# Layer two's second pass: one group of attention products for a block's four tiles in place of two groups for two tiles each

## The chip, the cores and the metric

The kernel runs on one core of one Trainium2 chip. The metric is the device time of one execution in microseconds; the time before is 2650.01 us, the median of three runs (2649.26 to 2651.77).

## What is computed

Two layers of an attention over small graphs: 128 graphs of S = 64 nodes with H = 768 features, all in float32.

```python
h = jnp.maximum(_layernorm(x), 0.0)
temper = sqrt(H)
for l in range(2):
    m_left  = einsum('bsh,oh->bso', h, W_left[l])
    m_right = einsum('bsh,oh->bso', h, W_right[l])
    u_left, u_right = h @ m_left.T / temper, h @ m_right.T / temper
    u = u_left * adj_tri + u_left * diag_mask + u_right * swapaxes(adj_tri, 1, 2)
    e = exp(u) * adj
    attention = e / (sum(e, axis=2) + 1e-10)
    h_lin = einsum('bsh,oh->bso', h, W_lin[l]) + b_lin[l]
    ctx = attention @ h_lin
    h = relu((ctx - mean(ctx)) / (std(ctx, ddof=1) + 1e-3) * ln_a[l] + ln_b[l])
out = x + h
```

## The kernel before

Each layer has two passes. The first makes the scores and the attention. The second, `pass_two`, makes `h_lin`, the attention products, the normalisation and, in layer two, the residual sum and the output. The change is in layer two's second pass.

**Blocks.** The 8192 rows are worked on in 16 blocks u of 512 rows: four tiles of 128 rows, called (r, k) with r and k 0 or 1, two graphs to a tile. `h_lin` of a block is computed by a bilinear scheme with fewer products than the plain one: 15 products (`ORDER`), each of eight matmuls of 128x128 by 256 columns (`multiply`, L1006). Their operands are sums of blocks of the weights, prepared once, and sums of blocks of the tokens (`T_SUMS`, 11 for each block, made on GpSimd at L245 for the next block).

**Banks and reads.** The products go to four PSUM banks named X, Y, Z and V. `NAME` turns them from one use to the next, so that the tile that TensorE's rows call Z can be the bank "X" of the order. Several products accumulate in one bank, and after each of them the running sum is read out into one or two of the six parts of the tile `hl`: the first read of a part is a copy on ScalarE (L300), every later one an addition on VectorE (L245, `hl<-hl,bank`). Products 0, 2, 4, 6, 8 and 10 share one bank, so each of them waits for the reads of the one before it there. Product 8 has two reads, both on VectorE. Four of the banks are loaded beforehand with the bias by ScalarE (`fresh`, L995).

**Order of the work.** Each engine has its own instruction stream in program order. All other work is hung on numbered slots: `put(n, f)` hangs a step on slot n, and `linear` runs slot 2i in the middle of product i and slot 2i + 1 behind its reads. Slots beyond 29 are carried into the next block, less 30. On the slots of a block u in layer two lie: the affine steps of the next block on ScalarE (L379, slots 9 to 14), the token sums of the next block on GpSimd (slots 15 to 27), and the finish of the block before. Block 15 is different: its products are run for tiles of r = 0 and then again for r = 1, with four matmuls each and 30 slots to each half.

**The finish before.** `finish(u, r)` finishes two tiles. `context` issues 16 matmuls of 64x64 by 384 columns (L1048) into two pairs of PSUM banks, `aux`. ScalarE squares both tiles with a running sum (L1193) and takes the root (L1195). Then come, on slots: `inverse` (VectorE, L1198 and L1199); `scaled` for each tile, a multiply by 1/deviation and by `a` on VectorE (L1203) and an addition of `b` on GpSimd (L1206); and `done` for each tile, a VectorE operation on two operands in SBUF, max(z, 0) + x (L1217), with two stores to the output on SP's queue (L1219). The rows of x come by `residual`, four loads on SP's queue (L1133) into two of four buffers `xr`. In blocks 1 to 14 of layer two the calls for (u - 1, 0) and (u - 1, 1) stand behind products 0 and 7, with their steps on slots 6 to 12 and 20 to 30.

**Layer one's finish.** `finish_block(u, more)` finishes all four tiles behind product 12. `context_block` issues 16 matmuls, eight of 512 and eight of 256 columns (L1071), into the `aux` banks and into two of the product banks. The two parts in product banks are copied to SBUF by VectorE (L1143), which frees them for the next block. Squares, deviation, inverse and scaled come on slots 25 to 36; in layer one scaled is on ScalarE (L1168), and the rows are then stored, with no done step.

`finish_last` makes the last two tiles of all, and `last_block` prepares rows for them, among others a negated `b` on GpSimd (L1093).

Of the kernel before, what the change touches and what calls it, by code (L numbers as in the profile page):

```python
# [12 lines left out]
AF = mybir.ActivationFunctionType  # L13
ALU = mybir.AluOpType
# [3 lines left out]
def kernel(  # L18
# [48 lines left out]
    def put(slot, *fs):  # L67
        plan.setdefault(slot, []).extend(fs)
# [943 lines left out]
    def pass_two(l, aside):  # L1012
        last = l == L - 1
        with tc.tile_pool(name=f"two{l}", bufs=2, reuse_waits="tile") as sp, \
# [59 lines left out]
            def batch(r, k, h):  # L1074
                return 4 * (h if k == 0 else 1 - h) + r + 2 * k
# [59 lines left out]
            def finish_block(u, more):  # L1135

                parts = context_block(u)
                tiles = ((0, 0), (0, 1), (1, 0), (1, 1))
                zs = {t: sp.tile([P, H], F32, name="z", bufs=4) for t in tiles}
                cut = (slice(0, T), slice(T, H))  # L1140

                for t in ((1, 1), (1, 0)):
                    nc.vector.tensor_copy(zs[t][:, cut[0]], parts[t][0])  # L1143
                    parts[t][0] = zs[t][:, cut[0]]
                    if t == (1, 1):
                        AHEAD.append(fresh(l, 0, more))
                ss = stat.tile([P, Q, 2], F32, name="ssb", bufs=2)
                sd = stat.tile([P, Q], F32, name="sdb", bufs=2)
                rs = stat.tile([P, Q], F32, name="rsb", bufs=2)

                def squares(t):
                    junk = zs[0, t[1]]
                    for n in range(2):
                        nc.scalar.activation(junk[:, cut[n]], parts[t][n], AF.Square,
                                             accum_out=ss[:, 2 * t[0] + t[1], n:n + 1])

                def deviation():
                    nc.vector.reduce_sum(sd, ss, axis=mybir.AxisListType.X)
                    nc.scalar.activation(sd, sd, AF.Sqrt, bias=floor, scale=1.0 / (H - 1.0))

                def inverse():
                    nc.vector.tensor_scalar_add(rs, sd, EPS_LN)
                    nc.vector.reciprocal(rs, rs)

                def scaled(t):
                    by = rs[:, 2 * t[0] + t[1]:2 * t[0] + t[1] + 1]
                    for n in range(2):
                        nc.scalar.activation(zs[t][:, cut[n]], parts[t][n], AF.Copy, scale=by)  # L1168
                    kept(u, *t, zs[t])

                order = ((1, 1), (1, 0), (0, 0), (0, 1))
                for f, slots in ((squares, (25, 26, 28, 29)), (scaled, (33, 34, 35, 36))):
                    for n, t in zip(slots, order):
                        put(n, lambda f=f, t=t: f(t))
                put(30, deviation)
                put(32, inverse)

            def kept(u, r, k, z):
                for h in range(PAIR):
                    nc.sync.dma_start(ROWS[u][batch(r, k, h)], z[h * S:(h + 1) * S])  # L1180

            def finish(u, r):

                cx = context(u, r)
                zs = [sp.tile([P, H], F32, name="z", bufs=4) for _ in range(2)]
                if last and not u and not r:
                    residual(u, r)
                two = "p (n d) -> p n d"
                ss = stat.tile([P, 2], F32, name="ss", bufs=2)
                sd = stat.tile([P, 2], F32, name="sd1", bufs=2)  # L1190
                rs = stat.tile([P, 2], F32, name="rs1", bufs=2)
                for k in range(2):
                    nc.scalar.activation(zs[k].rearrange(two, n=2), cx[k], AF.Square, accum_out=ss[:, k:k + 1])  # L1193

                nc.scalar.activation(sd, ss, AF.Sqrt, bias=floor, scale=1.0 / (H - 1.0))  # L1195

                def inverse():
                    nc.vector.tensor_scalar_add(rs, sd, EPS_LN)  # L1198
                    nc.vector.reciprocal(rs, rs)  # L1199

                def scaled(k):
                    if last:
                        nc.vector.scalar_tensor_tensor(  # L1203
                            zs[k].rearrange(two, n=2), cx[k], rs[:, k:k + 1],
                            rows["a"].rearrange(two, n=2), op0=ALU.mult, op1=ALU.mult)
                        nc.gpsimd.tensor_add(zs[k], zs[k], rows["b"])  # L1206
                        return
                    if (u, r, k) == (NB - 1, 1, 1):
                        nc.vector.tensor_scalar_mul(zs[k].rearrange(two, n=2), cx[k], rs[:, k:k + 1])
                    else:  # L1210
                        nc.scalar.activation(zs[k].rearrange(two, n=2), cx[k], AF.Copy, scale=rs[:, k:k + 1])
                    kept(u, r, k, zs[k])

                def done(k):
                    if last:
                        xs = XS[u, r]
                        nc.vector.scalar_tensor_tensor(xs[k], zs[k], 0.0, xs[k], op0=ALU.max, op1=ALU.add)  # L1217
                        for h in range(PAIR):
                            nc.sync.dma_start(out[u * NBB + batch(r, k, h)], xs[k][h * S:(h + 1) * S])  # L1219
                        if k and u + r < NB - 1 and (u, r) != (NB - 2, 0):  # L1220
                            residual(u + r, 1 - r)

                steps = [lambda f=f, k=k: f(k) for f in (scaled, done) for k in range(2)]
                return [inverse] + (steps if last else steps[:2])

# [35 lines left out]
            for u in range(NB):  # L1261
                turn = not last and u >= NB - 2
                put(4, lambda u=u: load_at(u))
                if u + 1 < NB:
                    load_h(2, l, u + 1, u == 0)
                    put_all(9 if u else 15, affine(2, l, u + 1))
                    put_sums_t((2, l, u + 1), 15 if u else 21, 1, 0)
                    if turn:
                        load_rows(1, 0, sp)
                        put_all(10, transpose_rows(1, 0, sp), 2)  # L1270
                        put(27, lambda: load_rows(1, 1, sp))
                    if u == 1 and not last:
                        sums_ahead(1, extra, 3)
                    assert not turn or not background
                    if u in aside:
                        aside[u]()
                    ends = {}
                    if u and last:
                        ends = {0: ((u - 1, 0), (6, 7, 8, 11, 12)), 7: ((u - 1, 1), (20, 21, 22, 30, 30))}
                    elif u > NB - 3:  # L1280
                        ends = {5: ((u - 1, 0), (16, 17, 18)), 11: ((u - 1, 1), (28, 29, 30))}
                    elif u:
                        ends = {12: (u - 1, None)}
                    linear(u, (0, 1), 0, ends, (0, 1) if u + 2 < NB else (0,))
                    for n in sorted(plan):
                        plan[n - 30] = plan.pop(n)
                else:
                    if turn:
                        load_h(1, 1, 0)
                        put_all(24, transpose_rows(1, 1, sp), 2)  # L1290
                        put_all(2, [fetch.popleft() for _ in range(8)], 2)
                        put_all(46, [lambda: TOKENS[1].step(0)] * Tokens.LIMIT, 1)
                        put(48, lambda: load_h(1, 1, 1))
                        put_all(28, affine(1, 1, 0), 3)
                        ends = ({1: ((u - 1, 0), (13, 14, 16)), 11: ((u - 1, 1), (34, 35, 36))},
                                {4: ((u, 0), (50, 51, 52))})
                    else:
                        last_block(u)
                        put(8, lambda: residual(u - 1, 1))
                        ends = ({0: ((u - 1, 0), (12, 13, 15, 19, 31)), 9: ((u - 1, 1), (28, 29, 30, 39, 41))},  # L1300
                                {2: ((u, 0), (44, 48, 51, 61, 62))})
                    linear(u, (0,), 0, ends[0], (1,))
                    linear(u, (1,), 30, ends[1], ())
                    for n in sorted(plan):
                        run(n)
                    for f in (finish_last if last else finish)(u, 1):
                        f()
# [57 lines left out]
```

## Time and profile before

| what | value |
|---|---|
| time, median of 3 runs | 2650.01 us |
| the profiled execution | 2648.42 us, of which 2646.6 us are the span from first to last instruction |
| granted TensorE clock, mean | 0.995 |
| busy: TensorE, VectorE, ScalarE, GpSimd | 2591.6, 1780.6, 935.4, 1763.1 us |
| layer two's second pass on TensorE | from about 2156 us to the end |

How rows are read: PE is TensorE, DVE VectorE, ACT ScalarE, POOL GpSimd, SP the engine whose queue issues DMAs. In a timeline a row has the start and the length in us, engine, line of the program, operation, out<-in, partitions x elements, the number of instructions merged in the row, and in brackets how long the engine had been idle before it and what ended that. In a group, `a/b/c` are the shortest, median and longest duration in ns.

### The profile page before, as it was taken

What the parts mean: (1) busy time and instruction counts of PE and PEld (TensorE: products, weight loads), DVE (VectorE), ACT (ScalarE), POOL (GpSimd) and SP (SyncE); (2) the same over time, 40 slices, a digit from 0 to 9 for tenths busy, and PEclk for the clock granted to TensorE, in tenths of its full rate; (3) what the DMA queues carried; (4) which work ended last, traced back from release to release, by engine and by line L of the source; (5) the groups of instructions that cost most, each with busy time, mean ns of one, the idle gap of its engine ahead of it and who ended that gap; (6) DMA issues with size and microseconds to landing.
All of it is one profiled execution on the core that took longest, in us unless ns stands there. A gap on an engine that the chain in (4) does not pass through costs nothing. (4 is left out here: it accounts for less than half of the span.)

```text
span 2646.6 us, 47202 instructions
## 1 busy us (share of the span) xinstructions
PE 2591.6 (98%) x18122; PEld 2217.1 (84%) x18122; DVE 1780.6 (67%) x2888; ACT 935.4 (35%) x1969; POOL 1763.1 (67%) x1392
## 2 busy tenths in 40 slices
PE   9899999999999999999999999999999989999998
PEld 8788888888888888888798888888888878887886
DVE  7878787777768445554456667677666676666667
ACT  5522223223113244454542222122222335555453
POOL 4766676666668657676276666667666657878786
PEclk9999999999999999999999999999999999999999
DMA  7443534343421354445794424253532215555655
GB/s 220 113 111 86 124 93 110 93 119 79 98 60 56 123 156 149 159 139 182 219 282 101 121 68 108 71 129 93 136 98 70 67 49 157 157 167 166 177 161 146
DMA packets 258465, 331.84 MB, mean 125 GB/s; under 512 B 56002, under 2 KB 190402, under 8 KB 258242
## 3 DMA queue, kind: packets, MB, share of 16 engines
q1 hardware_dynamic: 241442, 320.56, 44.3%
q10 hardware_dynamic: 16800, 8.26, 1.2%
q8 instruction: 145, 2.38, 0.4%
q14 instruction: 78, 0.64, 0.1%
HBM read 213.39 MB, written 115.34 MB: 124 GB/s over the span
## 5 line engine op out<-in xcount | busy, mean ns | idle before, releaser
L245 POOL TENSOR_TENSOR g<-ht 128x512 f32<-128x512 f32 (+1 forms) x620 | 785.9, 1279 | 420.8 <-PE Z L702 71.6
L245 POOL TENSOR_TENSOR g<-g,g 128x512 f32<-128x512 f32 (+1 forms) x310 | 397.9, 1291 | 136.7 <-PE C L702 22.0
L245 POOL TENSOR_TENSOR g<-ht,g 128x512 f32<-128x512 f32 (+1 forms) x272 | 346.1, 1282 | 164.8 <-PE Z L702 42.8
L702 PE MATMUL X<-g,g 128*128 128x256 f32 (+1 forms) x1080 | 252.9, 377 | 6.0 <-DVE m L914 6.0
L1006 PE MATMUL Z<-g,g 128*128 128x256 f32 x1024 | 244.1, 380 | 3.5 <-ACT hl L300 3.2
L702 PE MATMUL C<-g,g 128*128 128x256 f32 x1008 | 239.7, 381 | 4.9 <-POOL g L245 2.2
L702 PEld LDWEIGHTS X<-g,g 128*128 128x128 f32 x1080 | 203.0, 191 | 34.8 <-DVE m L914 6.8
L702 PE MATMUL Y<-g,g 128*128 128x256 f32 (+1 forms) x968 | 225.7, 376 | 3.8 <-POOL g L245 3.8
L1006 PEld LDWEIGHTS Z<-g,g 128*128 128x128 f32 x1024 | 191.6, 190 | 35.8 <-issue 4.1
L379 ACT ACTIVATE ht<-ht,b_col,a_col 128x256 f32<-128x256 f32 x384 | 196.1, 591 | 69.0 <-DMA ht<-h 53.8
L702 PEld LDWEIGHTS C<-g,g 128*128 128x128 f32 x1008 | 190.5, 190 | 32.9 <-POOL g L245 3.5
L702 PE MATMUL Z<-g,g 128*128 128x256 f32 (+1 forms) x936 | 217.0, 375 | 0.0
L702 PE MATMUL D<-g,g 128*128 128x256 f32 x880 | 209.8, 381 | 1.8 <-POOL g L245 1.8
L702 PEld LDWEIGHTS Y<-g,g 128*128 128x128 f32 x968 | 182.0, 190 | 27.8 <-POOL g L245 4.2
L702 PE MATMUL V<-g,g 128*128 128x256 f32 (+1 forms) x840 | 194.6, 375 | 3.1 <-POOL g L245 1.6
L702 PEld LDWEIGHTS Z<-g,g 128*128 128x128 f32 x936 | 174.5, 190 | 23.1
L702 PEld LDWEIGHTS D<-g,g 128*128 128x128 f32 x880 | 168.1, 191 | 25.7 <-POOL g L245 2.5
L1006 PE MATMUL X<-g,g 128*128 128x256 f32 x768 | 182.7, 379 | 0.0
L702 PEld LDWEIGHTS V<-g,g 128*128 128x128 f32 x840 | 157.6, 191 | 23.3 <-POOL g L245 1.7
L1206 POOL TENSOR_TENSOR z<-z,b 128x768 f32<-128x768 f32 x62 | 112.7, 1829 | 81.7 <-DVE z L1203 77.2
L245 DVE TENSOR_TENSOR m<-m,Y 128x512 f32<-128x512 f32 (+2 forms) x196 | 126.5, 667 | 58.4 <-ACT m L910 35.7
L245 DVE TENSOR_TENSOR m<-m,D 128x512 f32<-128x512 f32 x180 | 118.2, 677 | 70.0 <-ACT m L910 51.3
(222 smaller groups left out, 4612.0 us busy)
## 6 DMA issues: line engine op xcount, KB each, us to landing
ht<-h SPq DMA_DIRECT2D x126, 768.0 KB, 6.3
h<-xb SPq DMA_DIRECT2D x124, 384.0 KB, 6.6
z<-z SPq DMA_DIRECT2D x128, 192.0 KB, 3.1
x<-z SPq DMA_DIRECT2D x128, 192.0 KB, 5.4
xr<-in_x_dram SPq DMA_DIRECT2D x120, 192.0 KB, 3.8
out_dram<-xr SPq DMA_DIRECT2D x120, 192.0 KB, 2.7
x<-in_x_dram SPq DMA_DIRECT2D x112, 192.0 KB, 5.4
g<-form SPq DMA_DIRECT2D x40, 256.0 KB, 5.6
```

Source lines behind the costliest of these rows:

```text
L245: (eng.tensor_add if sign == "+" else eng.tensor_sub)(o, a, b)
L379: nc.scalar.activation(ht, ht, AF.Relu, bias=cols[1][:, c:c + 1], scale=cols[0][:, c:c + 1])
L702: nc.tensor.matmul(o, w[:, c, g * P:(g + 1) * P], t, start=(new and g == c == at == 0), stop=(c == K2 - 1), skip_group_check=True)
L1006: nc.tensor.matmul(p[:, n], b[t][:, c, r * P:(r + 1) * P], w[s][:, c, :], start=(i in FIRST and i not in PRELOAD and n == c == 0), stop=(c ...
L1206: nc.gpsimd.tensor_add(zs[k], zs[k], rows["b"])
```

## The change

In layer two, blocks 0 to 13 are finished by `finish_block` behind product 12 of the following block, as in layer one. `finish_block` gets layer two's steps: scaled is two VectorE operations a tile (512 and 256 columns) with `a`, followed by the addition of `b` on GpSimd, at slots 33, 35, 37 and 39; done is at slots 39, 41, 43 and 45, in the order (1,1), (1,0), (0,0), (0,1). The residual rows are loaded at slots 21 (r = 1) and 22 (r = 0) of the block that holds the group, and no longer inside `finish`. Block 14 is still finished by two calls of `finish` within block 15, now behind products 8 and 13 of its first half in place of 0 and 9, with other slots. Layer one is untouched.

```diff
@@ finish_block
+                def done(t):
+                    z, xs = zs[t], XS[u, t[0]][t[1]]
+                    nc.vector.scalar_tensor_tensor(xs, z, 0.0, xs, op0=ALU.max, op1=ALU.add)
+                    for h in range(PAIR):
+                        nc.sync.dma_start(out[u * NBB + batch(*t, h)], xs[h * S:(h + 1) * S])
+
                 def scaled(t):
                     by = rs[:, 2 * t[0] + t[1]:2 * t[0] + t[1] + 1]
                     for n in range(2):
-                        nc.scalar.activation(zs[t][:, cut[n]], parts[t][n], AF.Copy, scale=by)
-                    kept(u, *t, zs[t])
+                        if last:
+                            nc.vector.scalar_tensor_tensor(zs[t][:, cut[n]], parts[t][n], by, rows["a"][:, cut[n]],
+                                                           op0=ALU.mult, op1=ALU.mult)
+                        else:
+                            nc.scalar.activation(zs[t][:, cut[n]], parts[t][n], AF.Copy, scale=by)
+                    if last:
+                        nc.gpsimd.tensor_add(zs[t], zs[t], rows["b"])
+                    else:
+                        kept(u, *t, zs[t])
 
                 order = ((1, 1), (1, 0), (0, 0), (0, 1))
-                for f, slots in ((squares, (25, 26, 28, 29)), (scaled, (33, 34, 35, 36))):
+                steps = ((scaled, (33, 35, 37, 39)), (done, (39, 41, 43, 45))) if last else ((scaled, (33, 34, 35, 36)),)
+                for f, slots in ((squares, (25, 26, 28, 29)),) + steps:
@@ finish
-                if last and not u and not r:
-                    residual(u, r)
...
-                        if k and u + r < NB - 1 and (u, r) != (NB - 2, 0):
-                            residual(u + r, 1 - r)
@@ pass_two, blocks 1 to 14
                     if u and last:
-                        ends = {0: ((u - 1, 0), (6, 7, 8, 11, 12)), 7: ((u - 1, 1), (20, 21, 22, 30, 30))}
-                    elif u > NB - 3:
+                        for r in (1, 0):
+                            put(22 - r, lambda u=u, r=r: residual(u - 1, r))
+                    if u > NB - 3 and not last:
                         ends = {5: ((u - 1, 0), (16, 17, 18)), 11: ((u - 1, 1), (28, 29, 30))}
                     elif u:
                         ends = {12: (u - 1, None)}
@@ pass_two, block 15
                         last_block(u)
-                        put(8, lambda: residual(u - 1, 1))
-                        ends = ({0: ((u - 1, 0), (12, 13, 15, 19, 31)), 9: ((u - 1, 1), (28, 29, 30, 39, 41))},
+                        put(12, lambda: residual(u - 1, 0))
+                        put(17, lambda: residual(u - 1, 1))
+                        ends = ({8: ((u - 1, 0), (19, 20, 22, 26, 27)), 13: ((u - 1, 1), (31, 32, 34, 39, 41))},
                                 {2: ((u, 0), (44, 48, 51, 61, 62))})
```

## The prediction

> **What bounds the kernel now.** I read the page first, then TensorE's timeline over one block of layer two's second pass, then the same stretch on VectorE, GpSimd and ScalarE, and last a block of layer one's second pass, which already has the single group.
>
> ```profile
> PE 2591.6 (98%) x18122; PEld 2217.1 (84%) x18122; DVE 1780.6 (67%) x2888; ACT 935.4 (35%) x1969; POOL 1763.1 (67%) x1392
> ```
>
> TensorE is 98% busy, so only two things move the time: shorter TensorE work, or a new TensorE wait. One block (u around 10) of layer two on TensorE, first column the start, second the length:
>
> ```profile
> 2339.34 1.89 PE L1006 MATMUL Z<-g,g 128*128 128x256 f32 x8
> 2341.16 1.52 PE L1048 MATMUL aux<-hl,at 64*64 64x384 f32 x16
> 2342.61 1.99 PE L1006 MATMUL V<-g,g 128*128 128x256 f32 x8
> 2344.44 1.89 PE L1006 MATMUL Z<-g,g 128*128 128x256 f32 x8
> ...
> 2353.07 1.89 PE L1006 MATMUL X<-g,g 128*128 128x256 f32 x8
> 2354.89 1.52 PE L1048 MATMUL aux<-hl,at 64*64 64x384 f32 x16
> 2356.34 1.99 PE L1006 MATMUL Z<-g,ht 128*128 128x256 f32 x8
> 2358.17 1.89 PE L1006 MATMUL Y<-g,ht 128*128 128x256 f32 x8
> 2359.90 1.89 PE L1006 MATMUL Z<-g,g 128*128 128x256 f32 x8
> ...
> 2370.35 1.52 PE L1048 MATMUL aux<-hl,at 64*64 64x384 f32 x16
> ```
>
> No row has an idle time behind it: the pass is dense. Five products lie between 2344.44 and 2353.07, so one takes 1.726 us. The block repeats after 2370.35 - 2341.16 = 29.19 us; less 15 products that leaves 3.30 us for its two attention calls.
>
> **What is removed: TensorE time.** The single group as layer one runs it:
>
> ```profile
> 1087.06 1.89 PE L1006 MATMUL Y<-g,g 128*128 128x256 f32 x8
> 1088.88 0.65 PE L1071 MATMUL X<-hl,at 64*64 64x512 f32 x2
> ...
> 1089.79 1.90 PE L1071 MATMUL aux<-hl,at 64*64 64x256 f32 x24
> 1091.62 1.99 PE L1006 MATMUL V<-g,g 128*128 128x256 f32 x8
> 1093.45 1.89 PE L1006 MATMUL Y<-g,g 128*128 128x256 f32 x8
> ```
>
> From 1087.06 to 1093.45 are two products and the group: 6.39 - 3.45 = 2.94 us. It saves 3.30 - 2.94 = 0.36 us in each of the 14 blocks finished so (u = 0 to 13): **-5.0 us**. That is all the gain there is.
>
> **What moves: VectorE's part.** Before, a block's two scaled steps and two done steps come twice, in two places. Now four scaled come at slots 33 to 39 and four done at 39 to 45, that is at slots 3 to 15 of the block after the one that holds the group, without a pause. The rows that price them:
>
> ```profile
> 2348.77 1.94 DVE L1203 SCALAR_TENSOR_TENSOR z<-aux,rs,a 128x768 f32<-128x768 f32 x2
> 2351.62 0.69 DVE L245 TENSOR_TENSOR hl<-hl,Y 128x512 f32<-128x512 f32 x1 [0.91 <-PE Y L1006]
> 2352.22 4.00 DVE L1217 SCALAR_TENSOR_TENSOR xr<-z,xr 128x768 f32<-128x768 f32 x2
> 2358.45 1.29 DVE L245 TENSOR_TENSOR hl<-hl,Z 128x512 f32<-128x512 f32 x2 [2.23 <-PE Z L1006]
> L1217 DVE SCALAR_TENSOR_TENSOR xr<-z,xr x60: 951/2023/2432, 2206.2 to 2626.0; 128x768 f32<-128x768 f32 x60
> 2349.86 3.60 POOL L1206 TENSOR_TENSOR z<-z,b 128x768 f32<-128x768 f32 x2 [3.77 <-DVE z L1203]
> 2353.93 3.42 POOL L245 TENSOR_TENSOR g<-ht 128x512 f32<-128x512 f32 x2 [0.47 <-ACT ht L379]
> 2357.43 1.27 POOL L245 TENSOR_TENSOR g<-g,ht 128x512 f32<-128x512 f32 x1
> ```
>
> A done step needs 0.951 us alone (shortest of 60) but 2.02 in the median. The rows show why. The first was issued at 2352.22 while GpSimd's second z add ran (2349.86 + 3.60 = 2353.46); the sum that GpSimd began at 2353.93 then took far longer than 1.27, and the two dones ended at 2356.22. Taking turns gives just that: done from 2353.46 for 0.81, sum 1.13, done 0.81 = 2356.21. So where both queue, a done costs 0.81 plus what GpSimd has in hand: 1.13 for a sum, 1.68 for a z add. Steps with one operand in PSUM do not take part: scaled, L1203, is 1.94 for two beside an add, a read 0.69 beside a sum.
>
> The deadline is read 8. Products 8 and 10 accumulate in one bank, with both of product 8's reads on VectorE between them. Before, product 8 ends at 2358.17 (where product 9 starts), its two reads run 2358.45 to 2359.74, and product 10 starts at 2359.90: 0.16 us to spare, and VectorE had been idle 2.23 us.
>
> Now the chain after the change, from the start of a block's product 0, with 0.23 us from the end of a product to its read (the rows have 0.2 to 0.28), VectorE's next start 0.08 before the last end, and shorter pieces priced by two rows of a read:
>
> ```profile
> 2611.99 0.75 DVE L245 TENSOR_TENSOR hl<-hl,Z 128x256 f32<-128x256 f32 x2
> 2612.85 0.42 DVE L245 TENSOR_TENSOR hl<-hl,Y 128x256 f32<-128x256 f32 x1
> ```
>
> 0.69 at 512 columns and 0.42 at 256 is 0.27 for 256, so scaled in two pieces steps on by 0.66 + 0.40 us a tile from PSUM; the bottom tiles' first piece, copied to SBUF, by 0.60 (0.95 less 0.27, less 0.08).
> - Product 1 ends at 3.45, its read frees VectorE at 4.28. Bottom two tiles scaled: 6.28. Read 3 (product 3 ends 6.91): 7.74. Top two tiles: 9.86. First done is issued.
> - GpSimd adds from 5.44, the first held 0.4 by the second bottom tile: ends 7.64, 9.42, 11.20.
> - done 11.20 to 12.01; add 12.01 to 13.69 (read 5 meanwhile); done to 14.50; sum to 15.63; done to 16.44; sum to 17.57; done to 18.38.
> - Reads 8: 18.30 to 19.58; product 10 starts 19.68, where its turn is 10 x 1.726 = 17.26: **2.41 us late**, in every block from u = 2 to 14: 13 x 2.41 = **+31.3 us**.
>
> The same reckoning on the block before puts its done steps at 2340.17 and 2352.19, rows have 2340.14 and 2352.22, and no wait on TensorE.
>
> What of this price is not in the trace of before is the bottom scaled pieces: they have two SBUF operands, for the first time. By the row of L1203 they would not compete: then each later step comes 0.38 earlier, 14 x 0.38 = 5.4 us less, sum +27.7. By the row of L1217 they do: +33.1 as below. I take L1217's, whose operands they share.
> [...]
>
> **The last block** (u = 15) runs its tiles in two halves of 0.86 us a product. Block 13's scaled and done steps fall into its first half:
>
> ```profile
> 2602.11 1.03 PE L1006 MATMUL Z<-g,g 128*128 128x256 f32 x4
> 2608.83 2.13 POOL L1093 TENSOR_SCALAR nb<-b 128x768 f32<-128x768 f32 x1
> ```
>
> GpSimd's chain sets it: adds from 3.46, four of 1.78 and the negated row of 2.13, held some 1.8 by dones and a scaled, ends 14.5; two dones (1.7) and the reads bring product 10 to 16.97 instead of 10.30: **+6.65 us**, bounded below by 4.0 (nothing held). The later finishes of block 14, at products 8 and 13, then have VectorE to themselves about as before.
>
> **What is hidden.** ScalarE: squares in two pieces, after product 12, run where it was idle (6.73 us before 2341.32), and layer one shows the group without a wait behind its two copies (L1143, 0.69 for one). Its eight affine steps now meet product 8 without an attention call between:
>
> ```profile
> 2341.32 0.60 ACT L300 ACTIVATE hl<-Z 128x512 f32<-128x512 f32 x1 [6.73 <-PE Z L1006]
> 2349.82 0.60 ACT L300 ACTIVATE hl<-Z 128x512 f32<-128x512 f32 x1 [2.37 <-PE Z L1006]
> 2350.32 4.03 ACT L379 ACTIVATE ht<-ht,b_col,a_col 128x256 f32<-128x256 f32 x8
> 2354.25 0.58 ACT L300 ACTIVATE hl<-Z 128x512 f32<-128x512 f32 x1
> 1090.04 0.69 DVE L1143 COPY z<-Z 128x512 f32<-128x512 f32 x1 [0.36 <-PE Z L1071]
> ```
>
> Read 4 to the end of read 6 is 5.01 us; from 8.86 that is 13.87, and product 8's turn is 13.81: some 0.2 us late. Inside the 2.41 it costs nothing; in u = 1, which has no done steps yet, **+0.2**. DMA: outputs and residual rows change places on SP, where the next h loads stand behind them:
>
> ```profile
> ht<-h SPq DMA_DIRECT2D x126, 768.0 KB, 6.3
> out_dram<-xr SPq DMA_DIRECT2D x120, 192.0 KB, 2.7
> ```
>
> The last done at 18.4, its stores, and four residual loads let the h loads go at about 26 of 31 us; 6.3 later is 1 us into the next block, 8 before their first affine step. Nothing.
>
> **Sum:** 31.3 - 5.0 + 6.65 + 0.2 = +33.1 us. The profiled execution took 2648.42 us (2646.6 of span, 1.8 around it), the median is 2650.01. From the median: **2683 us**, from the profiled execution 2681.5. Own range: 5.4 less for the bottom tiles, 2.6 less for the last block, a tenth of a microsecond on each of four turns either way (0.4 x 14 = 6), and up to 1.7 more for the clock, which was granted at 0.83 in the 10 us that hold 3.8 us of TensorE idle, while the last block's wait is 6.65: 2669 to 2691.
>
> ```profile
> 87.00:97.00 10.00, 6.21 (x140) 5.34 (x144) 8.99 (x17) 1.81 (x4) 8.03 (x6) 0.83 0.04 9
> ```
>
> **Rivals.**
> - *The group pays and nothing else does* (faster): the dones end before product 8 does, at 15.5. That needs 2.9 us less than the chain has, and no late reads in the last block. For it: layer one's pass is dense with the same group. Against it: there the scaled step is ScalarE's and there is no done. 2650 - 5 = 2645.
> [...]
> - *More turns behind z adds* (slower still): should GpSimd run late, two more dones a block wait 1.68 in place of 1.13: 13 x 1.1 = 14 more, 2697. For it: four adds in a row, where before there were two.
>
> **How the numbers follow.** Forecast 0.74, faster 0.09, no change 0.06, slower still 0.11. A measurement can tell about 0.2%, 5.3 us. The faster case lies just at that bound (0.06 counted faster, 0.03 same), the no-change case half at each side (0.03 same, 0.03 slower). So faster 0.06, same 0.06, slower 0.88. The range, 2668 to 2699, takes the forecast's own and the slower case, rounded outwards by one and two, and leaves out the two of 0.15 together.
>
> **What would show it.** Right: blocks of about 31.2 us in layer two's second pass, one idle time a block on TensorE of about 2.1 to 2.4 us ahead of product 10, ended by VectorE's read; L1217's successor at 2 us in the median; a gap of 6 to 7 us in the last block; group 2.9 us. Wrong: TensorE dense with blocks of 28.8 us, done steps near 0.95 us, or the idle time at another product or ended by ScalarE, GpSimd or a DMA.

## The result, and the profile after

| | before | after |
|---|---|---|
| time, median | 2650.76 us (4 runs, 2649.26 to 2651.77) | 2683.86 us (4 runs, 2681.64 to 2687.09) |
| ratio to before | | 1.0124, 95% interval 1.0108 to 1.0140 |
| profiled execution, span | 2648.42, 2646.6 us | 2684.85, 2683.1 us |
| layer two's second pass, blocks u = 2 to 14 | 29.20 us each | 30.8 us each |

The change makes the kernel slower by 33.1 us; forecast were 33 (2683 us). Two lines of the page after say little of the cause: TensorE has 4.7 us more busy time, in a span that is 36.5 us longer.

```profile
span 2683.1 us, 47252 instructions
...
PE 2596.3 (97%) x18122; PEld 2220.2 (83%) x18122; DVE 1793.6 (67%) x2958; ACT 941.7 (35%) x2067; POOL 1772.6 (66%) x1392
```

TensorE's timeline over one block after, from product 0 to the group. Ahead of product 10 stands the only idle time, and a read on VectorE ended it:

```profile
2350.42 1.89 PE L1006 MATMUL Z<-g,g 128*128 128x256 f32 x8
...
2362.51 1.89 PE L1006 MATMUL X<-g,g 128*128 128x256 f32 x8
2364.31 1.99 PE L1006 MATMUL Z<-g,ht 128*128 128x256 f32 x8
2366.14 1.89 PE L1006 MATMUL Y<-g,ht 128*128 128x256 f32 x8
2369.57 1.99 PE L1006 MATMUL Z<-g,g 128*128 128x256 f32 x8 [1.53 <-DVE hl L245]
...
2375.85 1.90 PE L1071 MATMUL aux<-hl,at 64*64 64x256 f32 x24
```

Product 10 starts 19.15 us after product 0 (2350.42), where 17.26 was its turn: 1.89 us late. (The row gives 1.53: it counts from the end of product 9, which the profile only models, and products 7 and 8 had taken 0.18 more than their turn.) The block before it had its `aux` row at 2345.03, so the block repeats after 30.82 us.

VectorE over the same stretch, and GpSimd below it:

```profile
2354.70 0.69 DVE L245 TENSOR_TENSOR hl<-hl,V 128x512 f32<-128x512 f32 x1 [2.58 <-ACT hl L300]
2355.31 0.75 DVE L1175 SCALAR_TENSOR_TENSOR z<-z,rsb,a 128x512 f32<-128x512 f32 x1
...
2356.37 0.74 DVE L1175 SCALAR_TENSOR_TENSOR z<-z,rsb,a 128x512 f32<-128x512 f32 x1
...
2358.20 2.19 DVE L1175 SCALAR_TENSOR_TENSOR z<-aux,rsb,a 128x512 f32<-128x512 f32 x4
2360.31 1.08 DVE L1167 SCALAR_TENSOR_TENSOR xr<-z,xr 128x768 f32<-128x768 f32 x1
2361.31 0.67 DVE L245 TENSOR_TENSOR hl<-hl,Y 128x512 f32<-128x512 f32 x1
2361.91 6.41 DVE L1167 SCALAR_TENSOR_TENSOR xr<-z,xr 128x768 f32<-128x768 f32 x3
2368.24 1.27 DVE L245 TENSOR_TENSOR hl<-hl,Z 128x512 f32<-128x512 f32 x2
2356.53 9.03 POOL L1180 TENSOR_TENSOR z<-z,b 128x768 f32<-128x768 f32 x4 [6.58 <-DVE z L1175]
2365.51 3.94 POOL L245 TENSOR_TENSOR g<-ht 128x512 f32<-128x512 f32 x2
L1167 DVE SCALAR_TENSOR_TENSOR xr<-z,xr x56: 946/1978/2568, 2237.1 to 2642.8; 128x768 f32<-128x768 f32 x56
```

Three done steps in a row take 6.41 us, and only then come the two reads of product 8, which had ended when product 9 began, at 2366.14. At 2369.51 the reads end, at 2369.57 product 10 starts. The four additions on GpSimd take 9.03 us where four alone would take some 7.2. The two engines take turns: counted from the start of product 0, the additions end at 8.37, 10.14, 12.65 and 15.14 us, the done steps at 10.96, 13.46, 15.95 and 17.90. It is not that a done step waits for the result of its own addition: in every one of these blocks each done step begins at least 0.74 us after that has ended. The last row has the group of the done steps, shortest, median and longest in ns: 1978 in the median, close to the 2023 of before.

In the last block (u = 15) the wait is 6.00 us, and behind it the products, which elsewhere in that half have rows of 1.03 and follow each other after 0.86, are slow:

```profile
2637.30 1.13 PE L1006 MATMUL Y<-g,ht 128*128 128x256 f32 x4
2644.43 2.08 PE L1006 MATMUL Z<-g,g 128*128 128x256 f32 x4 [6.00 <-DVE hl L245]
2646.29 1.91 PE L1006 MATMUL X<-g,g 128*128 128x256 f32 x4
2648.00 1.91 PE L1006 MATMUL Y<-g,g 128*128 128x256 f32 x4
2649.71 1.34 PE L1006 MATMUL V<-g,g 128*128 128x256 f32 x4
...
2656.16 0.86 PE L1048 MATMUL aux<-hl,at 64*64 64x384 f32 x4
2657.42 1.51 PE L1048 MATMUL aux<-hl,at 64*64 64x384 f32 x12 [0.39 <-issue]
2640.30 3.41 DVE L1167 SCALAR_TENSOR_TENSOR xr<-z,xr 128x768 f32<-128x768 f32 x2 [2.30 <-POOL z L1180]
2644.40:2651.00 6.60, 6.58 (x20) 5.07 (x20) 4.71 (x10) 0.38 (x1) 3.62 (x2) 0.55 0.82 243
```

The last row is a window: its third number from the end is the granted clock, 0.55. These four products took 1.86, 1.71, 1.71 and about 1.2 us instead of 0.86 each. The row above it is VectorE's: here the third done step did wait for its own addition, 2.30 us, since GpSimd makes a row for the last tiles (L1093) between the four additions.

### The profile page after: what moved, and what is told of

The parts are those of the page before. It is cut to its first block, busy times and chain, and to the rows that moved or that the text cites. A ratio compares the mean times of both kernels' runs of the same rounds, so it can differ in the third digit from the quotient of the medians.

```text
span 2683.1 us, 47252 instructions
## 1 busy us (share of the span) xinstructions
PE 2596.3 (97%) x18122; PEld 2220.2 (83%) x18122; DVE 1793.6 (67%) x2958; ACT 941.7 (35%) x2067; POOL 1772.6 (66%) x1392
## 5 line engine op out<-in xcount | busy, mean ns | idle before, releaser
L245 POOL TENSOR_TENSOR g<-ht,g 128x512 f32<-128x512 f32 (+1 forms) x272 | 336.3, 1245 | 163.5 <-PE Z L702 43.7
L1180 POOL TENSOR_TENSOR z<-z,b 128x768 f32<-128x768 f32 x56 | 124.8, 2259 | 91.8 <-DVE z L1175 91.8
```

The lines of the kernel that those rows point to most:

```text
L245: (eng.tensor_add if sign == "+" else eng.tensor_sub)(o, a, b)
L1180: nc.gpsimd.tensor_add(zs[t], zs[t], rows["b"])
```

## The experiments

The theory: the done steps take turns with GpSimd, four of them stand ahead of product 8's reads in VectorE's queue, and product 10 waits for those. Rivals: the group itself or ScalarE holds TensorE; VectorE has too much work, whatever GpSimd does; the spacing of the steps counts, not their order. In an edit, `...` stands for code that is not shown.

**1. Without the done steps.**

```diff
 def done(t):
-    nc.vector.scalar_tensor_tensor(xs, z, 0.0, xs, op0=ALU.max, op1=ALU.add)
```

> The done step's VectorE operation is left out for the blocks that the group finishes (the max and the addition of z to x are not computed; the stores of xr stay). If the done steps ahead of read 8 hold product 10 (theory): TensorE dense again, blocks of 29.0 us as the one block without done steps has (29.02), no wait of 6 us in the last block, so about 2651 us, within 2 us of the kernel before. If the group itself, its copies or ScalarE's affine steps hold the product (rival): blocks stay at 30.8 us and the time at about 2684 us.

Measured: 2650.38 us, ratio to before 0.9998 (0.9989 to 1.0007). TensorE has no idle time in these blocks, and the group comes every 29.02 us:

```profile
2330.26 0.65 PE L1071 MATMUL X<-hl,at 64*64 64x512 f32 x2
...
2359.28 0.65 PE L1071 MATMUL X<-hl,at 64*64 64x512 f32 x2
...
2388.31 0.65 PE L1071 MATMUL X<-hl,at 64*64 64x512 f32 x2
```

So in these blocks neither the group nor ScalarE holds TensorE for more than the 0.2 us that the prediction gave them, and the group's own gain is 29.20 - 29.02 = 0.18 us a block. The wait ahead of product 10 hangs on the done steps. The last block does not hang on them alone: from its product 0 to the end it takes 48.17 us here, 44.53 before and 55.30 after. Of the 10.8 us that it lost, 3.6 stay without the group's done steps. Block 14's two finishes, which the change put later in it, are the likely reason; no run moves them alone.

**2. The last done step behind read 8.**

```diff
-... (done, (39, 41, 43, 45)) ...
+... (done, (39, 41, 43, 50 if u < NB - 3 else 45)) ...
```

> One step moved: the last of the four done steps at slot 50 in place of 45, behind the reads of product 8, for blocks 0 to 12; block 13 as it was, so the last block keeps its loss. If it is the queue ahead of read 8 that counts (theory): the last done has its 2 us in a place where nobody waits, blocks of 29.0 us in place of 30.8, 13 x 1.8 = 23 us gained, about 2660 us (the last block's loss of some 11 us less 0.2 x 14 of the group's gain, above 2650.8). [...]

Measured: 2658.22 us, ratio 1.0027 (1.0016 to 1.0039). One step of 0.95 us of work, moved, brings back 25.6 us; the blocks account for 13 x 1.78 = 23.1 of them. VectorE, the group on TensorE, and GpSimd:

```profile
2351.37 4.47 DVE L1167 SCALAR_TENSOR_TENSOR xr<-z,xr 128x768 f32<-128x768 f32 x2
2355.89 1.29 DVE L245 TENSOR_TENSOR hl<-hl,Z 128x512 f32<-128x512 f32 x2
2357.62 0.69 DVE L245 TENSOR_TENSOR hl<-hl,Y 128x512 f32<-128x512 f32 x1 [0.44 <-PE Y L1006]
2358.22 0.95 DVE L1167 SCALAR_TENSOR_TENSOR xr<-z,xr 128x768 f32<-128x768 f32 x1
2333.59 0.65 PE L1071 MATMUL X<-hl,at 64*64 64x512 f32 x2
...
2362.62 0.65 PE L1071 MATMUL X<-hl,at 64*64 64x512 f32 x2
2358.28 2.03 POOL L245 TENSOR_TENSOR g<-g,ht 128x512 f32<-128x512 f32 x1
```

The third done ends as the reads of product 8 come due, and the fourth now stands in the gap behind the read of product 9. There it was issued 0.06 us ahead of GpSimd's sum, took 0.95 and made the sum wait (2.03 for 1.27), which nobody waits for. Blocks are 29.03 us, and no wait comes back at another product, as it would if VectorE had too much work in a block; what is left above before is the last block, whose 6.00 us wait is still there.

**3. The last done step one slot later, but still ahead of read 8.**

```diff
-... (done, (39, 41, 43, 45)) ...
+... (done, (39, 41, 43, 46 if u < NB - 3 else 45)) ...
```

> The last done step at slot 46 in place of 45 for blocks 0 to 12: later by a slot, but still ahead of the reads of product 8 in VectorE's order. If only the order in VectorE's queue counts (theory): the wait stays, 2684 us, within 2. If the spacing of the steps counts (rival): some of the 23 us come back, 2660 to 2680 us.

Measured: 2680.90 us, ratio 1.0112 (1.0097 to 1.0127), which overlaps the interval of the change. The wait is the same, block by block:

```profile
2244.49 1.99 PE L1006 MATMUL Z<-g,g 128*128 128x256 f32 x8 [1.54 <-DVE hl L245]
2275.29 1.99 PE L1006 MATMUL Z<-g,g 128*128 128x256 f32 x8 [1.51 <-DVE hl L245]
2642.55 2.07 PE L1006 MATMUL Z<-g,g 128*128 128x256 f32 x4 [6.00 <-DVE hl L245]
2644.42 1.52 PE L1006 MATMUL X<-g,g 128*128 128x256 f32 x4
2645.78 1.03 PE L1006 MATMUL Y<-g,g 128*128 128x256 f32 x4
```

The median missed by 1 us (2684 within 2 was expected); the last three rows show one reason for it: behind the last block's wait two products were slow here, not four (1.87 and 1.36 us from start to start, where 0.86 is their turn). VectorE's 2958 instructions stand in exactly the same order in both kernels, and product 10 is as late: it starts 19.12 us after product 0 (2256.17 to 2275.29), 19.15 in the change. The run shows that a slot's number does nothing while the order in the queue stays. It does not test the rival: a wider spacing in the same order was not tried.

**4. Without GpSimd's additions.**

```diff
 if last:
-    nc.gpsimd.tensor_add(zs[t], zs[t], rows["b"])
```

> GpSimd's addition of b to z is left out for the blocks that the group finishes (b is not added there); VectorE's instructions and their order are untouched. If the done steps are long because they take turns with GpSimd (theory): their median falls from 1.98 to about 0.95 us, the four end before product 8 does, no wait, blocks of 29.0 us, the last block near its length before: 2650 us, within 3. If the four steps are late only because they stand in one clump with the scaled steps (rival): they start no earlier, so at least 1.2 of the 1.9 us stay in each block, 2670 us or more.

Measured: 2651.01 us, ratio 1.0004 (0.9994 to 1.0014). VectorE has the same instructions in the same order:

```profile
2350.26 0.95 DVE L1167 SCALAR_TENSOR_TENSOR xr<-z,xr 128x768 f32<-128x768 f32 x1
2351.12 0.68 DVE L245 TENSOR_TENSOR hl<-hl,Y 128x512 f32<-128x512 f32 x1
2351.72 2.69 DVE L1167 SCALAR_TENSOR_TENSOR xr<-z,xr 128x768 f32<-128x768 f32 x3
2356.36 1.29 DVE L245 TENSOR_TENSOR hl<-hl,Z 128x512 f32<-128x512 f32 x2 [1.95 <-PE Z L1006]
L1167 DVE SCALAR_TENSOR_TENSOR xr<-z,xr x56: 948/953/957, 2234.2 to 2611.7; 128x768 f32<-128x768 f32 x56
```

All 56 done steps take 0.95 us, three in a row 2.69 instead of 6.41, and VectorE is idle 1.95 us ahead of read 8. In the blocks, which take 29.02 us, the work on VectorE fits, and the turns with GpSimd do not. In the last block a wait of 1.33 us ahead of product 10 stays, out of 6.00.

**5 and 6. The last block mended, with the last done behind read 8 and without.** Block 13 is finished by two calls as before the change, in block 14, and the places of block 14's calls are moved ahead, together with the loads of the residual rows (not shown). The two kernels differ in one slot of the done steps (48 and 45).

```diff
+elif last and u == NB - 2:
+    ends = {7: ((u - 1, 0), (17, 17, 18, 27, 30)), 10: ((u - 1, 1), (24, 24, 24, 33, 37))}
...
-ends = ({8: ((u - 1, 0), (19, 20, 22, 26, 27)), 13: ((u - 1, 1), (31, 32, 34, 39, 41))},
+ends = ({2: ((u - 1, 0), (12, 13, 18, 25, 31)), 10: ((u - 1, 1), (25, 28, 28, 39, 39))},
```

> The group for blocks 0 to 12 with the last done at slot 48 (behind the reads of product 8), and block 13 finished by two calls as before, so that no four done steps fall into the first half of the last block. Theory: both losses are gone, the wait ahead of product 10 (13 x 1.8 us) and the last block's 11 us, and with them the half clock behind its 6 us wait; 13 blocks at 29.02 in place of 29.20 gain 2.3 us, which two crowded places (block 14, and the first half of the last block) take back by the same reckoning: 2651 us, from 2648 to 2653. Rival: the last block's loss comes from the later places of block 14's finishes and not from block 13's steps; then at least 5 us of it stay, 2654 us or more.

> As e4_last_block_two_calls, but the last done at slot 45 again: the last block is mended alone. Theory: the two losses add up, so the 12 blocks from u = 2 to 13 keep 1.8 us each and block 14 about as much: 2651 + 13 x 1.8 = 2674 us, from 2671 to 2677. Rival (the two are one loss carried along the queue): the wait ahead of product 10 changes with the end, below 2668 us.

Measured: 2652.14 us for the first, ratio 1.0001 (0.9992 to 1.0010), with before at 2652.09 in the same runs; 2672.94 us for the second, ratio 1.0080 (1.0065 to 1.0096). Mending the last block brings about 11 us (2683.86 to 2672.94 is 10.9; by the ratios, 0.0044 of 2651, 11.7). The done step is worth 20.8 us with the last block mended and 25.6 without, so the two losses add up to within some 5 us, which is within what these few runs can tell. That the last block's loss comes from block 13's steps alone is not shown, since both kernels move block 14's calls as well; experiment 1 is what divides it. The first kernel is the best version with the group, and it is level with the kernel before. The 13 x 0.18 us of gain are used up by its block 14, 32.45 us in place of 29.20, and by 0.7 us in the last block. In block 14 two finishes meet, and VectorE lets TensorE wait three times:

```profile
2590.14 0.86 PE L1048 MATMUL aux<-hl,at 64*64 64x384 f32 x4 [0.28 <-DVE z L1215]
2591.93 1.51 PE L1048 MATMUL aux<-hl,at 64*64 64x384 f32 x12 [0.93 <-DVE z L1215]
...
2599.70 1.97 PE L1006 MATMUL Y<-g,g 128*128 128x256 f32 x8 [0.89 <-DVE hl L245]
```

## Why the prediction was right, point by point

- **The group's gain.** Forecast: 0.36 us a block, 0.2 of it taken back by ScalarE ahead of product 8, 0.16 left. Measured: 0.18. ScalarE's part can be seen in the rows after: from 2362.51 to 2366.14 are products 7 and 8, 3.63 us instead of 3.45, 0.18 more.
- **The wait ahead of product 10.** The mechanism, place and releaser are as forecast, and experiments 1, 2 and 4 bear them out. Its size was 2.41 us forecast and 1.89 measured, outside the 2.1 to 2.4 that was named as a sign. The step that failed is "its read frees VectorE at 4.28": VectorE's read of product 1 waited for ScalarE's copy from the same product (2.58 <-ACT in its row) and freed VectorE at 2355.31, 4.89 after product 0. So the scaled steps and GpSimd's first addition came 0.6 later (6.11 for 5.44), while the first done, held by read 3, came when forecast (9.89 for 9.86). It therefore fell just ahead of the gap between the second and third addition and took 1.08 us, not 2.15. From there each turn had the price reckoned, 2.49 us behind an addition and 1.95 behind a sum, but two done steps stood behind a whole addition where one was forecast: they ended at 10.96, 13.46, 15.95 and 17.90 us (forecast 12.01, 14.50, 16.44, 18.38). That a later start of GpSimd made the wait shorter is luck of the order. The wait on ScalarE is in the trace of before, too, at the same read, and the prediction did not use it:

```profile
2345.31 0.69 DVE L245 TENSOR_TENSOR hl<-hl,V 128x512 f32<-128x512 f32 x1 [1.59 <-ACT hl L300]
```

- **Bottom scaled pieces.** Forecast: they take turns with GpSimd as the done steps do, and the second holds the first addition by 0.4 us. The rows agree: the second took its 0.74 us from 2356.37, and GpSimd's addition issued at 2356.53 ended only at 2358.79, after 2.26 us where the shortest of its group takes 1.79. Here, as with the done step of experiment 2 (0.95 us, and 2.03 for the sum issued 0.06 us later), the step issued first kept its time and the one behind it was longer. That two operands in SBUF decide it was a choice between two rows of before; no run changes the operands alone.
- **The last block.** Forecast +6.65 us; measured 25.63 us for the first half (2627.76 to 2653.39) in place of 16.44 (2602.11 to 2618.55), and 1.58 more from there to the end: +10.8. The wait itself was right: product 10 starts 16.67 us after product 0, forecast 16.97. The sum had left out the clock behind it, granted at 0.55, 3.0 us here (it was in the range at 1.7). And the step "the later finishes of block 14 ... then have VectorE to themselves about as before" failed: it put them at nothing, and experiment 1 has 3.6 us lost in the last block without block 13's done steps. In the change itself 1.58 us are seen, most of them in the attention call at 2656.16, whose last twelve matmuls start at 2657.42, 0.10 after VectorE's scaled step (L1215) has read the second `aux` tile of block 14's later finish. That this read held them is inferred from the times; the profile names no releaser.
- **The sum.** Blocks: 13 x 1.61 - 0.18 = 20.8 where 26.5 were forecast; last block 10.8 where 6.65 were. The two misses nearly cancel, 31.6 against 33.1; that the total came as close as it did is luck. The two profiled executions differ by 36.4 us, because the one after was already 4.7 us behind at the start of layer two's second pass, in code that is the same; the medians have 33.1.

The faster case, and that of no change, fell with the done steps' median of 1978 ns. The still slower one came in part: GpSimd's first addition started 0.67 us late and its last ended at 15.14, not 13.69, and one more done step than forecast stood behind a whole addition (0.55 us), but the first done step's earlier turn saved 1.07.

## What to carry to other kernels

A step's price depends on what another engine does at that moment: the done step costs 0.95 or 2.0 us with the same operands. Before steps are gathered in one place, look for the tightest deadline that stands behind them in the same queue (here two reads with 0.16 us to spare) and lay out both engines' turns by hand up to it; one step on the wrong side of that deadline cost 21 to 26 us. A layout that is good in one layer carries over only as far as its steps run on the same engines.

## What the runs showed of the hardware

After the 6.00 us wait of TensorE its granted clock was 0.55 over 6.6 us, and about 3.0 us were lost. In experiment 2, after the same wait, the four products took 1.87, 1.71, 1.70 and about 1.3 us, and the half 25.73; in experiment 3, after the same wait, the slow stretch cost 1.5 us (24.12 us for the half against 25.63). After the 1.5 us waits in the blocks the clock stayed at 1.00, in this block and in the twelve others:

```profile
2350.40:2381.20 30.80, 29.27 (x153) 23.66 (x152) 21.05 (x29) 15.49 (x40) 24.07 (x15) 1.00 0.56 157
```

So the 6.00 us wait had a price behind it as well, and it did not cost the same each time. What a wait between 1.5 and 6.00 us costs was not measured.
